# TensorE packing, a merged column sum and shifted copies in a scan, attention and convolution kernel

## The chip, the cores and the metric

The kernel runs on one core of a Trainium2 chip. The core has a matrix engine (TensorE, PE in the profile), a vector engine (VectorE, DVE), an activation engine (ScalarE, ACT), a general engine (GpSimd, POOL) and a queue engine (SyncE, SP). Each works through its own instructions in order; semaphores tie them together. DMA transfers are issued from the queues of POOL, SP and ACT. The metric is the device time of one execution in microseconds (us); the median of several runs is compared.

## The reference

Four layers are applied to an input of 8 images, 384 channels, 32 x 32 pixels, all in float32:

```python
# layer 0: normalise over channels, selective scan forwards and backwards, local gate
xn = x * rsqrt(mean(x*x, channels) + 1e-6) * norm_w
u, z = split(xn_flat @ in_proj.T);  u = silu(conv1d(u))
dt, Bm, Cm = split(u @ x_proj.T, [24, 40])
delta = softplus(dt @ dt_proj.T + dt_b)
h = exp(delta * A) * h + delta * u * Bm          # 16 states a channel, 1024 steps
y = (sum(h * Cm) + u * D) * silu(z);  g = y @ out_proj.T      # both directions
x = x + res_scale * (g * scale_mod + sigmoid(dwconv3(xn)) * xn)
# layer 1: conv branch, linear attention, MLP
x1 = conv1x1(dwconv3(conv1x1(x))) + x
qp, kp, v = phi(q(x1)), phi(k(x1)), v(x1)        # phi(t) = exp(t - t*t/2), 8 heads of 48
out = qp @ (kp.T @ v) / (qp @ sum(kp, pixels) + 1e-6)
x2 = x1 + proj(out);  x = x2 + mlp(layernorm(x2))
# layer 2: seven depthwise kernels (all fit into 13 x 13), summed
# layer 3: 1x1 conv + residual, 13 x 13 depthwise, gelu
```

## The kernel before, in words

The kernel is one program over all 8 images, in three stages.

**Rounds.** `_layers01` runs a loop over the images (line 1036). Round b runs the scan of image b (`scan`, line 678) and, between its 48 units, pieces of two generators: `front(b+1)` (line 554), all of layer 0 ahead of the scan for the next image, and `layer1(b-1)` (line 840), the whole of layer 1 for the image before. Round 0 has `fold()` beside it, round 1 `prepare()`, which builds the 13 x 13 kernels of the last two layers. Each `yield n` of a generator names a cost; the loop takes pieces in such a measure that all are used up when the scan ends (lines 1039, 1041, 1051: `front` counts 108, `layer1` 310). A planner (the tile framework) then fixes, ahead of the run and from its own estimates of durations, the order of the instructions on each engine: the earlier in the program, the higher the priority, among those that it takes to be ready. Buffers are handed out from pools of fixed size: 11 tiles `t2` of 128 x 512, three PSUM banks `mm` for short sums, three `mo` for long ones, two `acc` for the scan.

A scan unit is 4 exponentials on ACT (line 754), three passes of DVE over 128 x 2048 or 2052 elements (767, 691, and the scan itself in 774 or 777), and 8 matmul instructions on PE (693) that sum 4 states of 32 channels each in four column tiles of 32. A float32 matmul is two instructions.

The parts of the generators that the change touches:

- `front`, mean square: three squares on ACT, a matmul of each with `mean_w` (128 x 128, all 1/384, line 565), which leaves the mean on all 128 partitions; `rsqrt` (548) takes Ln and Exp on 128 x 512; DVE multiplies (570). `layer1` does the same for the variance (984 to 994).
- `front`, `xd`: for each direction d, three matmuls of 128 x 56 weights (637), a copy on ACT and a store of B and C. Then for each d three matmuls with only 24 contracted rows (650), Abs, Relu, Exp and Ln on ACT, and sums and stores (`deltas`, 663).
- `layer1`, k and v: for each 128 pixels, kp and vt are computed; four matmuls of 128 x 96 weights add v'k to the PSUM tile `kvs` (902), and three with a column of ones add the sums of kp in three further columns (906). `kv` and `ks` are read from `kvs` by DVE (912, 919).
- `layer1`, denominator: `den`, `rz` and `rzb` (951 to 965) on partitions 0 to 31.

**Convolutions.** `conv` (line 282) runs twice, as a and b, each time over 96 groups of 4 channels. Rows of 32 pixels of all 8 images lie behind each other in DRAM, with `PADW` zeros between them. For every four groups a tile `xt` (two buffers) is loaded by two POOL DMAs (295) of 64 partitions each: the same rows twice, the second shifted by one pixel, so that two horizontal taps are contracted in one matmul. For every two groups four DMAs of SP and ACT load the kernels `toep` (302). A group is 14 matmuls of 64 columns (312), into the two halves of one PSUM bank; `put2` (321) copies it out on DVE and ACT in turn and stores every four groups, `put3` (361) applies gelu on ACT and stores each group.

**Pointwise.** Between the two convolutions, 16 steps of a 1x1 conv (lines 336 to 357).

Of the kernel before, what the change touches and what calls it, by code (L numbers as in the profile page):

```python
# [39 lines left out]
PADW = KS - 1  # L40
# [23 lines left out]
def tile_layers(  # L64
# [39 lines left out]
    RL = PADW + B * (W + PADW)  # L104
# [144 lines left out]
    XL = RL - PADW // 2 - 6  # L249
    with tc.tile_pool(name="cw", bufs=1) as cwp, tc.tile_pool(name="cx", bufs=2) as cxp, tc.tile_pool(  # L250
# [31 lines left out]
        def conv(t_d, src_d, tag, put):  # L282

            xt = tp = None
            for g in range(NQ):
                if g % GB == 0:
                    xt = cxp.tile([P, 2 * GB, XL], FP, tag="xt", name=f"xt_{tag}_{g}")
                    for q in range(2):  # L290
                        src = bass.AP(
                            src_d.tensor, src_d[4 * g, 0, PADW - KS // 2 + q].offset,
                            [[RL, 2 * H], [2 * H * RL, 2 * GB], [1, XL]],
                        )
                        nc.gpsimd.dma_start(xt[2 * H * q : 2 * H * (q + 1)], src)  # L295
                ps = cps.tile([P, HALF], FP, tag="cv", name=f"cv_{tag}_{g}")
                if g % (GB // 2) == 0:
                    tp = toep[g // (GB // 2) % len(toep)]
                    for q in range(2):
                        for e in range(2):  # L300
                            lo = 2 * H * q + H * e
                            (nc.scalar if e else nc.sync).dma_start(
                                tp[lo : lo + H, :, e].rearrange("p g j t -> p g (j t)"),
                                t_d[2 * g : 2 * g + GB, lo : lo + H, :].rearrange("g p n -> p g n"),
                            )
                for t in range(KP // 2):
                    for e in range(2):
                        row = xt[:, 2 * (g % GB) + e, 2 * t : 2 * t + B * (W + PADW) - PADW]
                        rhs = bass.AP(
                            row.tensor, row.offset, [row.ap[0], [W + PADW, B], [1, W]]  # L310
                        )
                        nc.tensor.matmul(  # L312
                            ps[2 * H * e : 2 * H * (e + 1), 0:BW], tp[:, 2 * (g % (GB // 2)) + e, :, :, t].rearrange("p c j -> p (c j)"), rhs,
                            start=(t == 0), stop=(t == KP // 2 - 1), skip_group_check=True,
                        )
                put(g, ps[:, 0:BW])
# [19 lines left out]
        for t in range(H // 2):  # L336
            yt = cxp.tile([P, NC, NB], FP, tag="yp", name=f"yp_{t}", bufs=3)
            nc.sync.dma_start(yt, yf[:, :, t * NB : (t + 1) * NB])
            xo = xos[t % 3]
            for m in range(NC):  # L340
                ps = cps.tile([P, HALF], FP, tag="cv", name=f"pw_{t}_{m}")
                for k in range(NC):
                    nc.tensor.matmul(  # L343
                        ps[:, 0:NB], pwt[:, k, m * P : (m + 1) * P], yt[:, k, :],
                        start=(k == 0), stop=(k == NC - 1),
                    )
                tm = cxp.tile([P, NB], FP, tag="tm", name=f"tm_{t}_{m}", bufs=3)
                nc.scalar.activation(
                    tm, ps[:, 0:NB], AF.Identity, bias=pbias[:, m, :], scale=bns("pw", m)
                )  # L350
                for r in range(2):
                    mid = xo[:, m, r, PADW:RL].rearrange("p (b w) -> p b w", w=W + PADW)[:, :, 0:W]
                    nc.vector.tensor_add(
                        mid, tm[:, r * BW : (r + 1) * BW].rearrange("p (b w) -> p b w", w=W),
                        yt[:, m, r * BW : (r + 1) * BW].rearrange("p (b w) -> p b w", w=W),
                    )
            nc.gpsimd.dma_start(xf[:, :, 2 * t : 2 * t + 2, :], xo)  # L357
# [13 lines left out]
def _layers01(tc, nc, B, xv, x2_d, dram, ident, mean_w, eps5, eps6, one, half, minus1, vec, bns, bnt,  # L371
# [12 lines left out]
    with ExitStack() as ctx:  # L384
# [33 lines left out]
        wx = const(xproj_t.rearrange("(k p) e -> p k e", p=P), [P, NC, DTR + 2 * NST], "wx")  # L418
        wdt = const(dtproj_t, [DTR, C], "wdt")
# [7 lines left out]
        m8t = const(mask8_t, [32, C], "m8t")  # L427
# [22 lines left out]

        ones = wp.tile([P, 1], FP, tag="ones", name="ones")
        nc.vector.memset(ones, 1.0)
# [95 lines left out]
        def rsqrt(dst, ps, eps):  # L548
            nc.scalar.activation(dst, ps, AF.Ln, bias=eps)
            nc.scalar.activation(dst, dst, AF.Exp, scale=-0.5)  # L550
# [3 lines left out]
        def front(b):  # L554

            xn = []
            for h in range(2):
# [3 lines left out]
                stat = psum(f"ms_{b}_{h}")  # L561
                for c in range(NC):
                    sq = t2(f"sq_{b}_{c}_{h}")
                    nc.scalar.activation(sq, xh[:, c, :], AF.Square)
                    nc.tensor.matmul(stat, mean_w, sq, start=(c == 0), stop=(c == NC - 1))
                rstd = t2(f"rstd_{b}_{h}")
                rsqrt(rstd, stat, eps6)
# [43 lines left out]
            for h in range(2):  # L611
# [20 lines left out]
                xds = []  # L632
                for d in range(2):
                    xd = t2(f"xd_{b}_{h}_{d}")
                    ps = psum(f"xd_{b}_{h}_{d}")
                    for k in range(NC):
                        nc.tensor.matmul(
                            ps[: DTR + 2 * NST, :], wx[:, k, :], ucs[d][:, k, :],
                            start=(k == 0), stop=(k == NC - 1),
                        )  # L640
                    nc.scalar.copy(xd[: DTR + 2 * NST, :], ps[: DTR + 2 * NST, :])
                    nc.gpsimd.dma_start(bc_d[b, d][:, cols], xd[DTR : DTR + 2 * NST, :])
                    xds.append(xd)
                    yield 3

                for d in range(2):
                    dls, ts = [], []
                    for c in range(NC):
                        ps = psum(f"dt_{b}_{h}_{d}_{c}")
                        nc.tensor.matmul(  # L650
                            ps, wdt[:, c * P : (c + 1) * P], xds[d][:DTR, :], start=True, stop=True
# [11 lines left out]
                    def deltas(h=h, d=d, dls=dls, ts=ts, ucs=ucs):  # L663
                        for c in range(NC):
                            dl, t = dls[c], ts[c]
# [4 lines left out]
                        if d == 1:  # L670
                            for c in range(NC):
                                nc.vector.tensor_add(ucs[0][:, c, :], ucs[0][:, c, :], ucs[1][:, c, :])
                            nc.gpsimd.dma_start(udv[b][:, :, bass.ts(h, HALF)], ucs[0])

                    defer(1, deltas)
                    yield 6
# [163 lines left out]
        def layer1(b):  # L840
# [37 lines left out]

            wk = wtile(qkv_t[:, C : 2 * C], f"wk_{b}")
            wv = wtile(qkv_t[:, 2 * C : 3 * C], f"wv_{b}")  # L880
            kvs = long_psum(f"kvs_{b}")
            nc.tensor.matmul(kvs[:, 0 : C + NC], zero[:, 0:P], zero[:, 0 : C + NC], start=True, stop=False, skip_group_check=True)
            for t in range(L // P):
# [5 lines left out]
                for w, dst in ((wk, kp), (wv, vt)):  # L889
# [5 lines left out]
                    if w is wk:  # L895
                        phi(kp[:, :C], ps[:, :C], f"k_{b}_{t}")
                    else:
                        nc.scalar.copy(vt[:, :C], ps[:, :C])
                last = t == L // P - 1
                for a in range(NPR):  # L900
                    s = slice(a * PR, (a + 1) * PR)
                    nc.tensor.matmul(
                        kvs[:PR, s], vt[:, s], kp[:, s], start=False, stop=last, skip_group_check=True
                    )
                for c in range(NC):
                    nc.tensor.matmul(
                        kvs[:, C + c : C + c + 1], kp[:, c * P : (c + 1) * P], ones,
                        start=False, stop=last, skip_group_check=True,
                    )
# [6 lines left out]
            )  # L916
            ks = t2(f"ks_{b}")
            ksv = ks[:, 0 : NC * 32].rearrange("p (c e) -> p c e", e=32)
            nc.vector.tensor_mul(
                ksv, m8, kvs[:, C : C + NC].rearrange("p (c o) -> p c o", o=1).to_broadcast([P, NC, 32])  # L920
# [27 lines left out]
            for h in range(2):  # L948
                den = psum(f"den_{b}_{h}")
                for k in range(NC):  # L950
                    nc.tensor.matmul(
                        den[:32, :], ksv[:, k, :], qps[h][:, k, :], start=(k == 0), stop=(k == NC - 1)
                    )
                rz = t2(f"rz_{b}_{h}")
                nc.scalar.activation(rz[:32, :], den[:32, :], AF.Ln, bias=eps6[:32])
                nc.scalar.activation(rz[:32, :], rz[:32, :], AF.Exp, scale=-1.0)
                rzs.append(rz)
                yield 3
            for h in range(2):
                for k in range(NC):  # L960
                    ps = psum(f"rzb_{b}_{h}_{k}")
                    nc.tensor.matmul(
                        ps, m8t[:, k * P : (k + 1) * P], rzs[h][:32, :], start=True, stop=True
# [20 lines left out]
            for h in range(2):  # L984
                xn = xns[h]
                var = psum(f"var_{b}_{h}")
                for k in range(NC):
                    sq = t2(f"vs_{b}_{h}_{k}")
                    nc.scalar.activation(sq, xn[:, k, :], AF.Square)
                    nc.tensor.matmul(var, mean_w, sq, start=(k == 0), stop=(k == NC - 1))  # L990
                rstd = t2(f"rst1_{b}_{h}")
                rsqrt(rstd, var, eps5)
# [43 lines left out]
        for b in range(B):  # L1036
            work = []
            if b + 1 < B:
                work.append([front(b + 1), 108, 0])
# [114 lines left out]
```

## Time and profile before

| | us |
|---|---|
| median of 3 runs (6033.6 to 6047.84) | 6042.61 |
| the profiled execution | 6068.56 |
| its span, first to last instruction | 6066.8 |
| start to the first scan unit | 246 |
| round 0 | 492 |
| round 1 | 944 |
| rounds 2 to 6 (513, 558, 554, 550, 557) | 2732 |
| round 7 | 474 |
| layer 1 of the last image, alone | 366 |
| convolution a | 338 |
| pointwise | 138 |
| convolution b | 337 |

The stages are cut where the last `fr` of a round is computed (line 716) and where the first `xt` of a convolution is issued. PE is busy for 4850.3 us, DVE for 3998.1, ACT for 2852.0, POOL for 1216.0. In the lists of groups a line gives the source line, engine, operation, the tile written and read, the shape and the count; then busy time, the mean duration of one in ns, and the idle time of the engine just ahead of it with what ended it. PE's durations include its pipeline, so that consecutive matmuls overlap: how long a row of them takes is read from the start times in the timeline.

### The profile page before, as it was taken

Reading aid. Unit: us, or ns where it says so; the run is one execution under the profiler, and the core shown is the slowest. Engines: PE = TensorE matmul, PEld = TensorE weight load, DVE = VectorE, ACT = ScalarE, POOL = GpSimd, SP = SyncE. Lnnn points to the kernel's source line nnn. Section 1 sums busy time; section 2 is a strip of 40 time slices with the busy share of each in tenths; the row PEclk is TensorE's granted clock in tenths of the full one; section 3 lists DMA queues with packets and bytes.
Section 4 is the critical chain, followed back from the end, with each engine's and each line's share of the span. In section 5 each row is a group of like instructions: output and inputs, shape, how many; then the busy total and the mean of one; then the engine's idle time right before and its main releaser. Section 6 shows DMA issues by size and latency. Waiting matters only on the chain. (4 is left out here: it accounts for less than half of the span.)

```text
span 6066.8 us, 53234 instructions
## 1 busy us (share of the span) xinstructions
PE 4850.3 (80%) x19054; PEld 2142.6 (35%) x19054; DVE 3998.1 (66%) x2768; ACT 2852.0 (47%) x3941; POOL 1216.0 (20%) x1953
## 2 busy tenths in 40 slices
PE   3665546675479989898998999898978879798899
PEld 1121112222124324232333333242323324497488
DVE  0499995565674897998899789978989921000200
ACT  1555433443435755684577467556735513000211
POOL 4211111222122221212121121211110010211133
PEclk8676767787789989898999899898989979899999
DMA  8655554556473664567457556755663431598799
GB/s 284 202 181 178 181 187 135 167 171 186 139 224 117 192 203 147 170 203 211 143 181 212 157 183 184 213 151 165 199 171 111 142 95 47 111 221 192 220 217 196
DMA packets 429276, 1060.29 MB, mean 175 GB/s; under 512 B 61500, under 2 KB 111908, under 8 KB 429012
## 3 DMA queue, kind: packets, MB, share of 16 engines
q0 software_dynamic: 188640, 679.21, 39.0%
q1 hardware_dynamic: 210704, 354.31, 18.8%
q10 hardware_dynamic: 29668, 23.36, 1.6%
q8 instruction: 151, 2.47, 0.2%
q14 instruction: 113, 0.93, 0.1%
HBM read 807.16 MB, written 293.47 MB: 181 GB/s over the span
## 5 line engine op out<-in xcount | busy, mean ns | idle before, releaser
L754 ACT ACTIVATE da<-dlt,neg_a 128x512 f32<-128x512 f32 x1536 | 1005.2, 713 | 1061.3 <-DVE du L774 570.3
L767 DVE TENSOR_TENSOR du<-vr,bct 128x2048 f32<-128x2048 f32 x384 | 875.2, 2284 | 46.9 <-DMA vr<-v_d 41.0
L691 DVE TENSOR_TENSOR du<-du,bct 128x2048 f32<-128x2048 f32 x384 | 877.2, 2286 | 4.1 <-DVE xx L972 0.3
L777 DVE TENSOR_TENSOR_SCAN du<-da,du 128x2052 f32<-128x2052 f32 x192 | 848.8, 4427 | 13.9 <-ACT da L754 8.5
L774 DVE TENSOR_TENSOR_SCAN du<-da,du 128x2052 f32<-128x2052 f32 x192 | 848.0, 4426 | 8.5 <-ACT da L754 5.6
L693 PE MATMUL acc<-du,selt 128*32 128x512 f32 x3072 | 570.9, 687 | 324.2 <-DVE du L691 308.4
L1008 PE MATMUL mo<-hm,w 128*128 128x512 f32 x1152 | 568.0, 634 | 130.4 <-ACT hm L1006 129.3
L500 PE MATMUL mf<-ln,w 128*128 128x512 f32 x1152 | 552.3, 617 | 36.9 <-DMA w<-w_d 36.9
L1008 PEld LDWEIGHTS mo<-hm,w 128*128 128x128 f32 x1152 | 218.5, 200 | 474.8 <-issue 236.3
L500 PEld LDWEIGHTS mf<-ln,w 128*128 128x128 f32 x1152 | 214.9, 195 | 365.8 <-issue 326.2
L693 PEld LDWEIGHTS acc<-du,selt 128*32 128x32 f32 x3072 | 92.5, 115 | 681.8 <-DVE du L691 403.8
L312 PE MATMUL cv_b<-xt_b,toep 128*64 128x256 f32 x2688 | 304.5, 387 | 34.7 <-DMA xt_b<-xp_d 16.9
L509 PE MATMUL dw<-dw_i,t3b 96*32 96x512 f32 x1152 | 252.3, 784 | 99.0 <-DMA dw_i<-h_d 87.8
L312 PE MATMUL cv_a<-xt_a,toep 128*64 128x256 f32 x2688 | 302.9, 386 | 30.1 <-issue 24.2
L312 PEld LDWEIGHTS cv_b<-xt_b,toep 128*64 128x64 f32 x2688 | 291.6, 195 | 48.1 <-issue 33.5
L500 PE MATMUL in<-xn,win 128*128 128x512 f32 x576 | 284.2, 628 | 28.8 <-ACT uz L588 22.6
L312 PEld LDWEIGHTS cv_a<-xt_a,toep 128*64 128x64 f32 x2688 | 291.6, 195 | 41.1 <-issue 39.6
L754 ACT ACT_TABLE_LOAD x195 | 250.2, 1283 | 67.3 <-DVE du L777 41.1
L509 PE MATMUL lc<-lc_i,t 96*32 96x512 f32 x1152 | 188.4, 671 | 65.0 <-DMA lc_i<-xn_d 64.2
L1006 ACT ACTIVATE hm<-mf,biasf 128x512 f32<-128x512 f32 x192 | 129.9, 686 | 225.7 <-PE mf L500 224.3
L327 DVE COPY yt<-cv_a 128x256 f32<-128x256 f32 x48 | 20.4, 425 | 309.6 <-PE cv_a L312 309.6
L500 PE MATMUL h<-xx,c 128*128 128x512 f32 x288 | 143.6, 659 | 81.3 <-DMA xx<-x_d 81.3
(212 smaller groups left out, 6353.9 us busy)
## 6 DMA issues: line engine op xcount, KB each, us to landing
dlt<-dl_d SPq DMA_DIRECT2D x384, 256.0 KB, 5.3
vr<-v_d SPq DMA_DIRECT2D x384, 256.0 KB, 5.4
bct<-bc_d SPq DMA_DIRECT2D x256, 256.0 KB, 4.0
ut<-u_d POOLq DMA_DIRECT2D x192, 257.5 KB, 4.7
lc_i<-xn_d POOLq DMA_DIRECT2D x192, 228.8 KB, 4.6
dw_i<-h_d POOLq DMA_DIRECT2D x192, 228.8 KB, 4.2
tp_d<-g_d POOLq DMA_DIRECT2D x64, 672.0 KB, 9.4
w<-w_d POOLq DMA_DIRECT2D x64, 576.0 KB, 5.1
```

The lines of the kernel that those rows point to most:

```text
L312: nc.tensor.matmul(ps[2 * H * e : 2 * H * (e + 1), 0:BW], tp[:, 2 * (g % (GB // 2)) + e, :, :, t].rearrange("p c j -> p (c j)"), rhs, star ...
L327: nc.vector.tensor_copy(hold["t"][:, g % GB, :], ps)
L500: nc.tensor.matmul(ps, w[:, k, m * P : (m + 1) * P], rhs[k] if isinstance(rhs, list) else rhs[:, k, :], start=(k == 0), stop=(k == NC - 1),)
L509: nc.tensor.matmul(ps[32 * j : 32 * j + 32, :], lhs(j, i), rhs(j, i), start=(i == 0), stop=(i == taps - 1), skip_group_check=True,)
L691: nc.vector.tensor_mul(dv, dv, cct[:, 1:2, :].to_broadcast([P, 4, HALF]))
L693: nc.tensor.matmul(acc[32 * j : 32 * j + 32, :], selt, dv[:, j, :], start=False, stop=(r == NR - 1), skip_group_check=True,)
L754: nc.scalar.activation(da[:, SEG * j + 1 : SEG * (j + 1)], dlt[:, j, :], AF.Exp, scale=neg_a[:, 4 * c + j, r : r + 1],)
L767: nc.vector.tensor_mul(flat(1)[:, :, 0:HALF], vt, bct[r][:, 0:1, :].to_broadcast([P, 4, HALF]))
L774: nc.vector.tensor_tensor_scan(du[:, s], da[:, s], du[:, s], 0.0, ALU.mult, ALU.add)
L777: nc.vector.tensor_tensor_scan(du[:, s][:, ::-1], da[:, s][:, ::-1], du[:, s][:, ::-1], 0.0, ALU.mult, ALU.add)
L1006: nc.scalar.activation(hm, ps, AF.Gelu, bias=biasf[:, NC * i + f, :])
L1008: nc.tensor.matmul(acc[m], wb[:, f, m * P : (m + 1) * P], hm, start=(i == 0 and f == 0), stop=(i == FF // C - 1 and f == NC - 1),)
```

## The change

Four things are edited.

1. *Convolutions.* `PADW` falls from 12 to 6, so that neighbouring images share their padding, and a row has 312 elements instead of 364. `xt` is loaded by one DMA into one half of the partitions, and a DVE copy writes the other half, shifted by one element. Which half is loaded alternates (`flip`), and the kernels go to the matching halves.
2. *Mean squares and variances.* `rsqrt_mean` replaces `rsqrt`: twelve matmuls of 128 x 32 weights over 128 columns each put the mean of quarter j of the pixels on partitions 32j to 32j+31; Ln and Exp run on 128 x 128; four matmuls with `spread` bring each quarter back to all partitions, in PSUM, where DVE reads it.
3. *`xd` and `dt`.* The x_proj weights are padded to 64 columns. Both directions write one PSUM tile, in column tiles 0 and 64, and are copied in one go. `wdt` holds the dt weights twice, at partitions 0 and 64, so that the two directions' matmuls use different row tiles; the loop over chunks c is now outside the loop over d, with a yield of 3 for each c. `udv` is stored by chunk. `front` counts 90.
4. *Sums of k.* vt gets a 97th column of ones for each group of 96 (a memset on POOL), and the v'k matmul gives the sums in row 96. At the end of the image that row is copied by ACT, and three matmuls of one row turn it into columns. The denominator moves to partitions 32 to 63, with its mask in the free rows of `wdt`.

```diff
-PADW = KS - 1
+PADW = KS // 2
...
-    RL = PADW + B * (W + PADW)
+    RL = PADW + B * (W + PADW) + 2
...
-    XL = RL - PADW // 2 - 6
+    XL = RL - 1
...
-                    for q in range(2):
-                        src = bass.AP(
-                            src_d.tensor, src_d[4 * g, 0, PADW - KS // 2 + q].offset,
-                            [[RL, 2 * H], [2 * H * RL, 2 * GB], [1, XL]],
-                        )
-                        nc.gpsimd.dma_start(xt[2 * H * q : 2 * H * (q + 1)], src)
+                    flip = g // GB % 2
+                    src = bass.AP(
+                        src_d.tensor, src_d[4 * g, 0, 0].offset,
+                        [[RL, 2 * H], [2 * H * RL, 2 * GB], [1, XL]],
+                    )
+                    half0, half1 = (xt[2 * H * e : 2 * H * (e + 1)] for e in (flip, 1 - flip))
+                    nc.gpsimd.dma_start(half0, src)
+                    nc.vector.tensor_copy(half1[:, :, 0 : XL - 1], half0[:, :, 1:XL])
...
-        def rsqrt(dst, ps, eps):
-            nc.scalar.activation(dst, ps, AF.Ln, bias=eps)
-            nc.scalar.activation(dst, dst, AF.Exp, scale=-0.5)
+        def rsqrt_mean(srcs, eps, name):
+            stat = psum(f"{name}_s")
+            for k, src in enumerate(srcs):
+                for j in range(4):
+                    nc.tensor.matmul(
+                        stat[32 * j : 32 * j + 32, 0:P], mean_w[:, 0:32], src[:, j * P : (j + 1) * P],
+                        start=(k == 0), stop=(k == NC - 1), skip_group_check=True,
+                    )
+            r = t2(f"{name}_r")[:, 0:P]
+            nc.scalar.activation(r, stat[:, 0:P], AF.Ln, bias=eps)
+            nc.scalar.activation(r, r, AF.Exp, scale=-0.5)
+            ps = psum(f"{name}_b")
+            for j in range(4):
+                nc.tensor.matmul(
+                    ps[:, j * P : (j + 1) * P], spread[:, j, :], r, start=True, stop=True,
+                    skip_group_check=True,
+                )
+            return ps
...
-                xds = []
-                for d in range(2):
-                    xd = t2(f"xd_{b}_{h}_{d}")
-                    ps = psum(f"xd_{b}_{h}_{d}")
-                    for k in range(NC):
+                xd = t2(f"xd_{b}_{h}")
+                ps = psum(f"xd_{b}_{h}")
+                for k in range(NC):
+                    for d in range(2):
+                        nc.tensor.matmul(
+                            ps[64 * d : 64 * d + 64, :], wx[:, k, :], ucs[d][:, k, :],
+                            start=(k == 0), stop=(k == NC - 1), skip_group_check=True,
+                        )
+                nc.scalar.copy(xd, ps)
...
+                for c in range(NC):
+                    dls, ts = [], []
+                    for d in range(2):
+                        ps = psum(f"dt_{b}_{h}_{d}_{c}")
+                        at = slice(64 * d, 64 * d + DTR)
                         nc.tensor.matmul(
-                            ps, wdt[:, c * P : (c + 1) * P], xds[d][:DTR, :], start=True, stop=True
+                            ps, wdt[at, c * P : (c + 1) * P], xd[at, :], start=True, stop=True
                         )
...
-                        nc.scalar.copy(vt[:, :C], ps[:, :C])
+                        vv1 = vt[:, : C + NPR].rearrange("p (a e) -> p a e", e=PR + 1)
+                        nc.gpsimd.memset(vv1[:, :, PR : PR + 1], 1.0)
+                        nc.scalar.copy(
+                            vv1[:, :, 0:PR], ps[:, :C].rearrange("p (a e) -> p a e", e=PR)
+                        )
...
-                        kvs[:PR, s], vt[:, s], kp[:, s], start=False, stop=last, skip_group_check=True
-                    )
-                for c in range(NC):
-                    nc.tensor.matmul(
-                        kvs[:, C + c : C + c + 1], kp[:, c * P : (c + 1) * P], ones,
-                        start=False, stop=last, skip_group_check=True,
+                        kvs[: PR + 1, s], vv1[:, a, :], kp[:, s], start=False, stop=last,
+                        skip_group_check=True,
                     )
...
+            nc.scalar.copy(kv[PR : PR + 1, :C], kvs[PR : PR + 1, :C])
+            kss = psum(f"kss_{b}")
+            for c in range(NC):
+                nc.tensor.matmul(
+                    kss[:, c : c + 1], kv[PR : PR + 1, c * P : (c + 1) * P], spread[PR : PR + 1, 3, 0:1],
+                    start=True, stop=True, skip_group_check=True,
+                )
...
-                work.append([front(b + 1), 108, 0])
+                work.append([front(b + 1), 90, 0])
```

## The prediction

> **What bounds the kernel now.** I read first the busy time by stage, then, inside one steady round and inside a convolution, the waits and the timeline, then the rows of the instructions that change. By stage (us; busy time and instructions of PE, weight loads, DVE, ACT, POOL; granted clock, DMA share, GB/s): round 0, one steady round, convolution b.
>
> ```profile
> 246.00:738.00 492.00, 291.22 (x975) 87.73 (x976) 480.62 (x309) 271.71 (x392) 84.63 (x151) 0.67 0.53 177
> 2753.00:3307.00 554.00, 492.78 (x1654) 179.44 (x1650) 492.65 (x316) 356.95 (x479) 113.00 (x193) 0.93 0.60 182
> 5730.00:6067.00 337.00, 304.47 (x2688) 291.56 (x2688) 0.00 (x0) 45.55 (x96) 117.70 (x144) 0.97 0.96 202
> ```
>
> Round 0 is DVE from end to end. In a steady round PE and DVE are both busy for 89%, so each bounds for a part. Where PE bounds is seen in the timeline of that round, DVE's long stalls first, then PE while k'v is summed:
>
> ```profile
> 2857.47 0.69 DVE L873 TENSOR_TENSOR xx<-xx,c 128x512 f32<-128x512 f32 x1 [6.38 <-ACT c L870]
> 2889.03 0.17 DVE L764 COPY du<-carry 128x4 f32<-128x4 f32 x1 [15.42 <-PE acc L693]
> 2921.01 0.17 DVE L764 COPY du<-carry 128x4 f32<-128x4 f32 x1 [4.21 <-PE acc L693]
> ...
> 2879.17 0.92 PE L902 MATMUL kvs<-kp,vt 128*96 128x96 f32 x8
> 2879.93 0.76 PE L906 MATMUL kvs<-ones,kp 128*128 128x1 f32 x6
> 2880.54 1.54 PE L892 MATMUL kv_kp<-wk,xx 128*128 128x384 f32 x4
> 2887.90 1.07 PE L693 MATMUL acc<-du,selt 128*32 128x512 f32 x8
> ```
>
> From 2850 to 2943 PE has hardly a gap, and DVE waits some 25 us there for sums queued behind other PE work. Of the round's 61 us of DVE idle time, the list of waits puts only 23 on `acc`; later stretches (3060 to 3307, where `xd` and `dt` lie) have DVE busy and PE with short gaps. Rows that change:
>
> ```profile
> L650 PE MATMUL dt<-xd,wdt 24*128 24x512 f32 x192 | 106.2, 668 | 5.6 <-DVE biasf L824 5.5
> L637 PE MATMUL xd<-uc,wx 128*56 128x512 f32 x192 | 95.3, 623 | 7.3 <-ACT uc L630 7.3
> L565 PE MATMUL ms<-sq,mean_w 128*128 128x512 f32 x96 | 56.3, 730 | 66.9 <-ACT sq L564 63.4 <-DVE bias L824 3.3
> L906 PE MATMUL kvs<-ones,kp 128*128 128x1 f32 x384 | 48.3, 241 | 0.0
> ```
>
> In convolution b, four groups take PE 12.49 us, and the second of the two row loads is issued 6 us after the first:
>
> ```profile
> 5806.41 0.69 POOL L295 DMA_DIRECT2D xt_b<-xp_d  x1 [1.61 <-PE cv_b L312]
> 5807.09 0.89 POOL L364 DMA_DIRECT2D out<-ot  x1
> 5807.36 12.49 PE L312 MATMUL cv_b<-xt_b,toep 128*64 128x256 f32 x112 [1.25 <-ACT ot L363]
> 5812.42 0.69 POOL L295 DMA_DIRECT2D xt_b<-xp_d  x1
> 5820.19 12.49 PE L312 MATMUL cv_b<-xt_b,toep 128*64 128x256 f32 x112 [0.34 <-issue]
> ```
>
> POOL holds the second load behind two stores of `out`; with 8.0 us to landing (median of these loads) it arrives at about 5820, when PE starts again. PE runs from 5739.2 to 6061.6, 322 us, where 24 x 12.5 = 300 would do; in convolution a from 5265.2 to 5586.9, also 322. The DMA engines are 0.96 and 0.89 busy.
>
> [...] the 8 scan instructions above, four tiles of 32, take 0.99 us to the next start, about as long as two unpacked ones (0.89); no run here shows row tiles. [...]
>
> **The change part by part.** The sum is made against the profiled execution, 6068.56 us, 2 us more than its span and 26 more than the median of the runs; the difference is then taken from the median.
>
> *Convolutions.* Bytes for four groups: rows 2 x 704 KB, now 64 x 8 x 311 x 4 = 622 KB; the kernels stay at 8 x 112. So 2304 KB become 1518, and one POOL issue of 0.69 us goes. New is the DVE copy of 64 x 8 x 310 = 2480 elements a partition: [...] I take 1.45. [...] The four groups in the other buffer hide it for 12.5. In convolution a, `put2` copies are queued behind it on DVE; six PSUM banks, 19 us of groups, cover that wait. Without cover the stall would be the copy, 24 x 1.45 = 35 us a convolution. [...] I leave 0.1 us a tile: 322 becomes 303, 19 saved, twice. The first tile of each: 10.6 and 9.8 us from issue to first matmul now, some 2 less with one load. Together -42. What is late next is PE itself.
>
> *Sums of k.* 64 pixel blocks lose 6 instructions, 0.61 us between starts: 39 us of PE. In the steady rounds this lies in the stretch that PE bounds: 8 x 0.61 = 4.9 a round. Added: 64 memsets on POOL, 0.22 us each by the memsets of line 522, before the ACT copy of vt. If a memset were late, vt, then `kvs`, then the sums behind it would be. POOL waits 9 to 14 us for `z_d` there; but what PE does later cannot stand ahead of a memset that PE's earlier sum needs, so I take 0, with 0 to 1 us a block (64) as bounds. Per image one ACT copy (0.47 as line 932) and six tiny matmuls follow; the projection of kv does not wait for them: 0 to 1.
>
> *`xd` and `dt`.* `xd`: six instructions take 2.66 us (3090.9 to 3093.6), 32 times, 85 us; halved, -43. `dt`: 96 matmuls of about 0.95, -46 if row tiles pair, 0 if not. But DVE bounds that stretch: 0 on the path. ACT gets 6 table loads a half image instead of 4, 32 x 1.28 = 41 us, about 5 a round beside 357 busy of 554; DVE waited 2.0 for `da` in that round. 0, at worst +5 a round. 32 more POOL issues of 0.55 lie on an engine 20% busy.
>
> *Mean squares.* 2.66 us of PE become 24 short instructions, 0.75 to 1.5, and 8 with a full weight load, 0.1 each as in line 906: 1.6 to 2.3; 32 times, -10 to -35, taken -20. ACT's two passes fall from 0.69 and 0.63 to about 0.37 and 0.31 (slope from 384 and 512 elements, 612 and 714 ns). New is that PE, not only DVE, waits for them:
>
> ```profile
> 740.28 1.28 ACT L549 ACT_TABLE_LOAD   x1
> 741.58 0.69 ACT L549 ACTIVATE rstd<-ms,eps 128x512 f32<-128x512 f32 x1
> 742.28 1.28 ACT L550 ACT_TABLE_LOAD   x1
> 743.58 0.63 ACT L550 ACTIVATE rstd<-rstd 128x512 f32<-128x512 f32 x1
> ```
>
> Two loads and two short passes make 3.3 us between `stat` and `spread`. Everything on PE behind `spread` waits unless the planner puts other matmuls in between; in the steady round the matmuls of `h` and `in` stand there now, in a place that they may keep. I take 1 us a round uncovered.
>
> *Sum.* Convolutions -42. PE loses 39 + 43 + 46 + 20 = 148 us of work; on the path: rounds 2 to 6, (4.9 - 1) x 5 = -20; round 1 -6; rounds 0 and 7 -2; last layer 1 alone, -5 + 1 = -4; shorter padding to clear, -1. Total -75: 6068.6 gives 5993.6, the median 6042.6 gives **5968**.
>
> **Rivals.** *Rounds unmoved*: DVE, at 89%, takes nothing of PE's gain; only -42, 6000. For it: most PE savings lie where DVE is busy. Against: 25 us of DVE waiting in the k'v stretch. *PE is the bound*: all 148 and the convolutions count, 6042.6 - 190 = 5853. Against: round 0 and the later half of each round. *Packing does nothing*: row tiles don't pair; that costs 46 us of PE but none of the path, 5970. *Slower, the spread wait*: 32 times PE stands from `stat` to the end of Exp, 3.3 us bare, 6 with four exponentials of the scan (2.6) ahead in ACT's queue. All uncovered, 32 x 6 = 192: 6042.6 - 75 + 192 = 6160. It decides from 75/32 = 2.3 us a time. For it: PE works in order, and in rounds with no gap the scan's sums, then DVE, stand behind it. *Order drawn anew*: round 1 takes 944 us with PE 563 and DVE 629 busy, since the order fixed ahead keeps engines waiting in turn; other piece sizes change every order. Either sign, 30 to 100 us.
>
> **How the numbers follow.** The sum as worked out, paired row tiles or not, 0.40; rounds unmoved 0.17; PE bound or a luckier order 0.11; slower by the spread wait or the order 0.26; gain and loss cancelling 0.06. Three runs spread over 14 us, so 0.2%, 12 us, is about what a measurement can tell. Faster 0.68, same 0.06, slower 0.26. The sum's own range is 5930 to 6010; with rivals of both signs, and the bounds of memsets (+64) and table loads (+35), 5865 to 6110.
>
> **What would show it.** PE in each convolution within 305 us, the copy row near 1.45 us, DMA share below 0.8. Line 906 gone. `xd` at half its PE time. Round 0 unchanged; steady rounds 545 to 553. Wrong if PE shows waits of over 2 us for Exp ahead of `spread`, if vt's copy waits for a POOL memset, or if round 1 leaves 900 to 970.

## The result

The changed kernel takes 6054.62 us (median of 4 runs, 6039.45 to 6061.74), the kernel before 6040.34 in the same comparison (4 runs, 6033.6 to 6047.84): ratio 1.002, 95% interval 0.9997 to 1.0043. That is no change that can be measured. The forecast was 5968. The two profiled executions are the other way round, 6068.56 before and 6039.45 after: the first lies above every timed run of its kernel, the second is the fastest of its own. So stages are read from them for what happens inside, and sums are taken from medians.

The stages of the changed kernel that answer to those shown of before: round 0 (cut, as before, just ahead of the first scan instruction), one steady round, convolution b (columns: start and end, length; busy time and instructions of PE, weight loads, DVE, ACT, POOL; granted clock, DMA share, GB/s).

```profile
232.00:724.00 492.00, 272.25 (x1028) 81.61 (x1025) 468.94 (x304) 270.80 (x384) 88.22 (x159) 0.68 0.53 176
2729.00:3292.00 563.00, 482.62 (x1720) 179.97 (x1720) 491.02 (x315) 354.61 (x477) 116.46 (x207) 0.92 0.58 181
5720.00:6038.00 318.00, 305.37 (x2688) 282.69 (x2688) 37.82 (x24) 45.54 (x96) 108.98 (x120) 0.98 0.71 154
```

Convolution b has lost 19 us, as forecast, with a DMA share of 0.71 instead of 0.96. Round 0 is as long as before. The steady round has 10 us less PE work (482.6 against 492.8) and the same DVE work, and is 9 us longer, not shorter. The gain of both convolutions is there; it is given back in the rounds.

Groups of the changed kernel, in the form of the groups shown of before:

```profile
L316 PE MATMUL cv_b<-xt_b,toep 128*64 128x256 f32 x2688 | 305.4, 389 | 14.0 <-DVE xt_b L298 14.0
L298 DVE COPY xt_b<-xt_b 64x2480 f32<-64x2480 f32 x24 | 37.8, 1576 | 263.5 <-DMA xt_b<-xp_d 263.5
L673 PE MATMUL dt<-xd,wdt 24*128 24x512 f32 x192 | 86.1, 684 | 20.4 <-ACT dl L678 7.3 <-DVE fr L737 5.5 <-DMA x_d<-xx 5.5
L658 PE MATMUL xd<-uc,wx 128*64 128x512 f32 x192 | 60.4, 605 | 1.2 <-ACT uc L651 1.2
L931 PE MATMUL kvs<-kp,vt 128*97 128x96 f32 x512 | 59.0, 260 | 41.9 <-ACT vt L925 30.0 <-POOL vt L924 11.4
L570 PE MATMUL ms_b<-ms_r,spread 128*128 128x128 f32 x128 | 27.7, 384 | 58.4 <-ACT ms_r L567 58.4
```

PE waits in convolution b only for the first copy (14.0 us). `xd` falls from 95.3 to 60.4 us of PE, and the product of 97 rows costs what that of 96 did (260 ns against 255 before). `dt` falls less, from 106.2 to 86.1, because only about half of its 48 pairs (the matmuls of the two directions for one chunk) start together. In the timeline of PE in the same round:

```profile
3264.22 1.12 PE L673 MATMUL dt<-xd,wdt 24*128 24x512 f32 x2
3270.03 1.13 PE L673 MATMUL dt<-xd,wdt 24*128 24x512 f32 x4
```

Four instructions (both directions) take as long as two (one direction): two row tiles do run at once, where the planner leaves them side by side.

### The profile page after: what moved, and what is told of

Same layout as the page of the kernel before. It is cut to its first block, busy times and chain, and to the rows that moved or that the text cites. A ratio compares the mean times of both kernels' runs of the same rounds, so it can differ in the third digit from the quotient of the medians.

```text
span 6037.7 us, 54476 instructions
## 1 busy us (share of the span) xinstructions
PE 4758.3 (79%) x19550; PEld 2101.6 (35%) x19550; DVE 4065.4 (67%) x2815; ACT 2851.9 (47%) x3949; POOL 1212.2 (20%) x2006
## 3 DMA queue, kind: packets, MB, share of 16 engines
q1 hardware_dynamic: 210704, 354.31, 19.5%
## 4 chain that ended last, share of the span: by engine, by line
PE 28%; DVE 24%; issue 23%; DMA 11%; ACT 7%; POOL 4%; SPq 1%; POOLq 0%; DVEq 0%; ACTq 0%
DVE du L798 7%; DVE du L788 6%; DVE du L795 6%; PE cv_a L316 5%; DVE du L712 3%; PE mo L1038 3%; PE mf L508 3%; DMA vr<-v_d 2%; PE in L508 2%; PE acc L714 2%; DMA x_d<-fr 2%; DMA dl_d<-dl 1%; POOL out L368 1%; PE c L508 1%; DMA dw_i<-h_d 1%
## 5 line engine op out<-in xcount | busy, mean ns | idle before, releaser
L714 PE MATMUL acc<-du,selt 128*32 128x512 f32 x3072 | 583.4, 702 | 372.3 <-DVE du L712 357.7
L1038 PE MATMUL mo<-hm,w 128*128 128x512 f32 x1152 | 586.4, 652 | 110.2 <-ACT hm L1036 109.5
L298 DVE COPY xt_b<-xt_b 64x2480 f32<-64x2480 f32 x24 | 37.8, 1576 | 263.5 <-DMA xt_b<-xp_d 263.5
```

Source lines behind the costliest of these rows:

```text
L714: nc.tensor.matmul(acc[32 * j : 32 * j + 32, :], selt, dv[:, j, :], start=False, stop=(r == NR - 1), skip_group_check=True,)
L1038: nc.tensor.matmul(acc[m], wb[:, f, m * P : (m + 1) * P], hm, start=(i == 0 and f == 0), stop=(i == FF // C - 1 and f == NC - 1),)
```

## The experiments

Each kernel was timed beside the kernel before, in five comparisons; it ran 4 to 22 times, and the medians of the kernel before lie between 6035.5 and 6040.2.

### One part at a time

**Convolutions alone.** The kernel before with the row loading and the padding of the change.

```diff
-PADW = KS - 1
+PADW = KS // 2
...
+                    nc.gpsimd.dma_start(half0, src)
+                    nc.vector.tensor_copy(half1[:, :, 0 : XL - 1], half0[:, :, 1:XL])
```

> The kernel before with the new loading of the convolution rows alone (one row load, the copy shifted by one on VectorE, shorter padding); everything between is as before. Theory A (the convolutions gained what was forecast, the rounds gave it back): 6040 - 36 to 42, that is 5998 to 6004, with each convolution at 304 us from first to last matmul. Theory B (the convolutions' gain is not real, since their stages in the changed kernel only look shorter): 6035 to 6045.

Measured: 6083.46, ratio 1.0072 (1.0059 to 1.0084). Both theories fall. Each convolution is 305 or 306 us on PE, as wanted, and the whole is 47 us slower. From the end of round 0 to the first row load of convolution a, the profiled execution takes 4582 us where the kernel before takes 4515.

**The packing alone.** The changed kernel with the old convolutions and the old padding.

```diff
-PADW = KS // 2
+PADW = KS - 1
...
-                    nc.gpsimd.dma_start(half0, src)
-                    nc.vector.tensor_copy(half1[:, :, 0 : XL - 1], half0[:, :, 1:XL])
```

> The changed kernel with the old convolutions: all the packing between the scan rounds, none of the row loading. Theory A: the packing as a whole costs what the convolutions gained, 6080 to 6100. Theory B: the packing is neutral, 6040 +- 12.

Measured: 6028.51, ratio 0.9983 (0.9974 to 0.9992). The packing between the rounds is worth 8 us. So it isn't what gave the gain back: the convolution edit is.

**Sums of k alone.** Lines 904 to 953 of the changed kernel, with a small tile of ones in place of `spread`.

```diff
+                        nc.gpsimd.memset(vv1[:, :, PR : PR + 1], 1.0)
-                for c in range(NC):
-                    nc.tensor.matmul(
-                        kvs[:, C + c : C + c + 1], kp[:, c * P : (c + 1) * P], ones,
```

> The kernel before with k's sums taken in the v'k product alone (a memset of ones in vt, product of 97 rows, six tiny matmuls per image in place of 384 one-column matmuls). The forecast's step (4.9 us a round in five rounds, some in round 1): 6010 to 6020. Rival 1 (the product now waits for vt, some 4.6 us a round in place of the gain): 6035 to 6045. Rival 2 (the waits for vt cost more than the sums): 6055 to 6080.

Measured: 6013.83, ratio 0.9962 (0.9949 to 0.9975): 23 us less, in the range of the forecast's step.

**Means alone.** The denominator moves to partitions 32 to 63 with them.

```diff
-                rsqrt(rstd, stat, eps6)
+                rstd = rsqrt_mean(sqs, eps6, f"ms_{b}_{h}")
```

> The kernel before with the mean squares and reciprocal roots alone done in the packed way (means in four column tiles, exponential on one row of four, spread back by four short matmuls); the mask of the denominator moves into rows 32 to 64 of the dt weights' tile to make room. Theory 1 (the wait ahead of the spread gives the gain back): 52 us of PE waits for it in rounds 2 to 6 of the changed kernel, less some 13 us of PE work saved there: 6070 to 6090. Theory 2 (these waits are only other waits under a new name, since the mean's own PE work shrank): 6030 to 6045. The forecast's step: 6035 to 6045.

Measured: 6049.59, ratio 1.0018 (1.0008 to 1.0029): 13 us slower, below what theory 1 asks and above theory 2. Its 22 runs spread from 6027 to 6069, wider than those of any other kernel here.

**`xd` and `dt` alone.**

```diff
-                for d in range(2):
+                for c in range(NC):
...
-                work.append([front(b + 1), 108, 0])
+                work.append([front(b + 1), 90, 0])
```

> The kernel before with xd and dt alone done in the packed way (both directions in two column tiles and two row tiles, chunks outside the loop over directions, the denominator on partitions 32 to 63). The forecast: none of its PE saving on the path, 6030 to 6045. If the parts of the packing add up (the packing as a whole -8, k's sums -23, the means +13): 6038. Rival (the two more table loads a half image are on the path): 6055 to 6075.

Measured: 6041.18, ratio 1.0006 (0.9997 to 1.0014). Nothing, as forecast; the 25 more table loads (666 against 641 in all) don't show. The three parts add up to -23 + 13 + 2 = -8, as much as the packing measures as a whole.

### Which part of the convolution edit: loading or layout

In the kernel with the convolution edit alone the instructions of PE, ACT and SP stand in the same order as in the kernel before, one by one (PE's neighbours in different tiles, which run side by side, as the eight of a scan unit do, 0.99 us to the next start in the kernel before, start up to four places apart); DVE has only the copies added, and on POOL a few issues near 90 us, ahead of round 0, have changed places. The order of work can't be the cause. What is left: the new loading reaches back, or the rows of `x2_d`, which layer 1 writes in every round and which are now 312 elements long instead of 364, with 6 zeros between images instead of 12.

```diff
 PADW = KS - 1
 RL = PADW + B * (W + PADW)
...
+                    nc.gpsimd.dma_start(half0, src)
+                    nc.vector.tensor_copy(half1[:, :, 0 : XL - 1], half0[:, :, 1:XL])
```

> The kernel before with one row load and the shifted copy, but with the old padding of 12 and the old row length of 364. Theory A1 (the new row layout slows the stores of layer 1's output, 32 runs of 128 bytes in each DMA packet, and through them the rounds): the rounds stay as in the kernel before and the convolutions gain, 5995 to 6005. Rival A2 (something in the new loading itself reaches back into the rounds): about 6080 as the full convolution edit.

```diff
-PADW = KS - 1
+PADW = KS // 2
...
                     for q in range(2):
                         nc.gpsimd.dma_start(xt[2 * H * q : 2 * H * (q + 1)], src)
```

> The kernel before with the new padding of 6 and row length of 312, but with two row loads as before. Theory A1: the rounds of the full convolution edit, some 65 to 70 us longer, with convolutions near the old 322 us (12% fewer bytes, a few us less): 6090 to 6110. Rival A2: 6030 to 6040.

Measured: new loading on old rows 5996.11, ratio 0.9934 (0.9916 to 0.9952); new rows with the old loading 6077.27, ratio 1.0071 (1.0054 to 1.0089). The loading is worth 39 us. The row layout costs 83 us with the new loading (1.0072 against 0.9934). Convolution b of the kernel with new rows and old loads (the same columns as above) shows why its total is lower than was expected:

```profile
5758.00:6073.00 315.00, 296.50 (x2688) 289.03 (x2688) 0.00 (x0) 45.50 (x96) 118.23 (x144) 0.98 0.94 204
```

With 12% fewer bytes in the row loads, and two of them, it is as short (301 us from the first matmul to the last) as with one load on old rows. Either half of the edit frees the convolutions, so this kernel shows the cost of the rows less that gain.

How the layout costs time is seen in POOL's timeline at the end of round 5. First new loading on old rows, then the full convolution edit:

```profile
3828.44 3.50 POOL L1024 DMA_DIRECT2D x_d<-xx  x3 [1.98 <-DVE xx L1021]
3841.26 0.56 POOL L721 DMA_DIRECT2D x_d<-fr  x1 [1.75 <-DVE fr L720]
3846.88 0.75 POOL L849 DMA_DIRECT2D xx<-x_d  x1 [5.06 <-DMA x_d<-fr]
```

```profile
3871.81 3.50 POOL L1024 DMA_DIRECT2D x_d<-xx  x3 [1.98 <-DVE xx L1021]
3884.64 0.56 POOL L721 DMA_DIRECT2D x_d<-fr  x1 [1.75 <-DVE fr L720]
3897.98 0.76 POOL L849 DMA_DIRECT2D xx<-x_d  x1 [12.78 <-DMA x_d<-fr]
```

In both, the first line is three stores of layer 1's output to `x2_d` (each is 2048 runs of 32 pixels, 128 bytes; the last three of the kernel before went out in 192 packets of 4096 bytes, 32 runs each). The last `fr` of the round is stored 12.8 us later, and then POOL waits for it to land, since layer 1 of the next image reads it back as `xx`. On old rows the wait is 5.1 us, on new rows 12.8: a store of `fr` that is issued behind slow stores lands late itself. What PE pays, in the lists of waits from round 1 into the last layer 1, in the same order of kernels:

```profile
PE h L504 <- DMA xx<-x_d: 78.7, 8, 15.4
PE c L513 <- DMA ut<-u_d: 1.4, 1, 1.4
PE ms L569 <- ACT sq L568: 7.1, 2, 6.7
```

```profile
PE h L504 <- DMA xx<-x_d: 116.3, 7, 20.8
PE c L513 <- DMA ut<-u_d: 29.2, 4, 10.1
PE ms L569 <- ACT sq L568: 17.6, 2, 14.9
```

(Columns: us in total, times, the longest.) These three grow by 38, 28 and 11 us, and the list as a whole from 785 to 855, while the stretch up to convolution a grows from 4501 to 4582 us. All are loads that land late, the third by way of `xi`, which the squares read (ACT waits 39 us for it instead of 30).

### Alignment or row length

The stores of `x2_d` in the kernel with the full convolution edit, image by image (windows around the six stores of images 1, 3, 4 and 7 in turn; columns: count, KB each, median us from issue to landing):

```profile
x_d<-xx POOLq DMA_DIRECT2D x6, 256.0 KB, 13.7
x_d<-xx POOLq DMA_DIRECT2D x6, 256.0 KB, 6.3
x_d<-xx POOLq DMA_DIRECT2D x6, 256.0 KB, 17.3
x_d<-xx POOLq DMA_DIRECT2D x6, 256.0 KB, 6.0
```

Images 0, 2, 5 and 6 have 19.5, 14.3, 16.2 and 13.6. In the same windows the stores of `fr` land in 5.3 us behind image 3 and in 14.1 to 18.6 behind images 1, 2, 4 and 5. The run (32 pixels) of image b begins 24 + 152b bytes into a row, and a row has 1248 bytes, a multiple of 32. So, if the tile itself begins at a multiple of 32 bytes, all runs of images 3 and 7, and of no other image, do so too. In the changed kernel, with the same rows, images 3 and 7 have 7.4 and 6.0, the others 11.3 to 22.7. In the kernel before (48 + 176b, rows of 1456) one run in two is aligned, in every image: 9.2 to 15.2 us. If alignment is the cause, a padding of 8 (32 + 160b, rows of 1312) repairs all images, and a padding of 16 puts every run at a multiple of 64.

```diff
-PADW = KS // 2
+PADW = 8
-    RL = PADW + B * (W + PADW) + 2
+    RL = PADW + B * (W + PADW)
-    XL = RL - 1
+    XL = B * (W + PADW) - PADW + KS
-                        src_d.tensor, src_d[4 * g, 0, 0].offset,
+                        src_d.tensor, src_d[4 * g, 0, PADW - KS // 2].offset,
```

> The changed kernel with a padding of 8 instead of 6 (row length 328), so that each run of 128 bytes in the rows of layer 1's output starts at a multiple of 32 bytes, half of them at one of 64. Theory A1 in the form that alignment is the cause: the rounds of the packing alone with old rows, or better, and the new convolutions: 5960 to 5990. Rival A3 (the row pitch or the place in DRAM is the cause, not the alignment): 6030 to 6060, like the changed kernel.

> The changed kernel with a padding of 16 (row length 400), every run of 128 bytes at a multiple of 64 bytes. If 64 bytes are the unit that matters: 5950 to 5980 and shorter packets than with padding 8. If 32 bytes are: within 8 us of padding 8, a little above it for the longer row loads and copies (3040 elements a partition instead of 2480). Rival A3: 6030 to 6060.

Measured: padding 8: 5953.57, ratio 0.9866 (0.9841 to 0.9891); padding 16: 5958.38, ratio 0.9878 (0.9855 to 0.99). The changed kernel with nothing but this padding is 1.3% faster than the kernel before. Rival A3 falls. The order of work is not a rival here: the packing alone, the changed kernel and these two share one order, up to the same small swaps as above; the kernel before, both halves of the convolution edit, the edit as a whole and the convolutions with a padding of 8 (below) share another. 32 bytes are enough: with padding 16 the stores take 7.1 us to land, with padding 8 (stores of rounds 2 to 6):

```profile
x_d<-xx POOLq DMA_DIRECT2D x30, 256.0 KB, 7.0
x_d<-fr POOLq DMA_DIRECT2D x30, 256.0 KB, 5.4
```

In the changed kernel as it is these two lines read 17.1 and 16.3. The waits appear at other places than in the convolution edit alone, since the order of work is another one. Waits of PE and DVE in rounds 1 to 7 of the changed kernel, first with a padding of 8, then as it is:

```profile
PE ms_s L561 <- ACT sq L587: 20.0, 8, 6.7
PE acc L769 <- DMA y<-ud_d: 17.9, 6, 7.6
DVE du L788 <- DMA vr<-v_d: 21.9, 9, 7.5
```

```profile
PE ms_s L561 <- ACT sq L587: 51.9, 7, 13.4
PE acc L769 <- DMA y<-ud_d: 44.2, 8, 15.5
DVE du L788 <- DMA vr<-v_d: 50.1, 12, 16.4
```

These waits grow by 32, 26 and 28 us. The second and third are loads that land late. The first is a store: a square takes the buffer of a `dl` tile whose store to `dl_d` has not landed; ACT waits 33 us for that in three places, and with a padding of 8 not at all.

The boundary of 32 bytes is what these runs show, for the start of each run in an ordinary store: in the kernel with the full convolution edit, 6.0 to 6.3 us for aligned runs of 128 bytes, 13.6 to 19.5 for unaligned ones. The size of the runs costs little here: with a padding of 8, aligned runs of 128 bytes land in 7.0 us where the 2048-byte rows of `fr`, in stores of the same 256 KB, take 5.4. What fills the extra time of an unaligned store, no run shows.

### What the packing is worth on aligned rows

Three kernels with a padding of 8: the convolutions alone; with k's sums; with k's sums, `xd` and `dt` (the changed kernel without its packed means).

> The kernel before with the new row loading and a padding of 8: no packing. If alignment is worth as much to the old rounds as to the packed ones (5954 against 6028 less 38): 5996 - 37, that is 5950 to 5970. If the old rounds, which have another order of work, hide more of it: 5975 to 5995.

> As the last, with k's sums in the v'k product too. If both gains add: 5930 to 5945, below every kernel so far. If the gain of k's sums was in the same waits that alignment removed: 5950 to 5965.

> The changed kernel with a padding of 8 and without the packed means (mean squares and reciprocal roots as before). If the packed means cost 13 here too: 5940 against 5954 with them. If they cost only in the old order of work: 5950 to 5960. Against the kernel without the packing of xd and dt it tells what that is worth in this place; forecast 0.

Measured: 5967.26 (0.9889, 0.9872 to 0.9905); 5946.81 (0.9848, 0.9835 to 0.9862); 5916.41 (0.9802, 0.9781 to 0.9822). Against old rows, alignment is worth 5996 - 5967 = 29 us without any packing. K's sums give 20 again. `xd` and `dt`, worth nothing before, are worth 30 here, and the means cost 5954 - 5916 = 37. Neither was forecast. The sums of k hardly change the order of the rest: of 18142 matmul instructions that both kernels have, 526 stand more than four places away.

### The packed means: wait or order

With a padding of 8, first only the front's means packed, then only those of layer 1, then both with a fixed tile in place of the exponential's result (this edit is shown; it leaves out the use of the means):

```diff
-                    ps[:, j * P : (j + 1) * P], spread[:, j, :], r, start=True, stop=True,
+                    ps[:, j * P : (j + 1) * P], spread[:, j, :], mean_w, start=True, stop=True,
```

> The changed kernel with a padding of 8, and of the packed means only those of the front (layer 0's mean square); layer 1's variance as before. Between 5916 (no packed means) and 5954 (both). If the cost lies in the wait ahead of the spread: the front's spreads waited 41 us in rounds 2 to 6 of the kernel with both, layer 1's 14, so three quarters of the 37 here: about 5944. If the order of work is the cause: anywhere between, not in proportion to the waits.

> The same with the packed variance of layer 1 alone. By the waits: 5916 plus a quarter of 37, about 5926. If the order of work is the cause: not in proportion.

> The changed kernel with a padding of 8, in which the spread multiplies a fixed tile of 128 x 128 instead of the exponential's result: all instructions are there, but PE has nothing to wait for at the spread (what is left out is the use of the computed means). If the wait is the cause of the 37: 5910 to 5925. If the order of work, or the work itself, is: 5940 to 5960; but the planner also draws the order anew, so that only a value near 5954 speaks clearly.

Measured: 5935.06 (ratio 0.9828, 0.9815 to 0.9842), 5965.01 (0.9876, 0.9863 to 0.989) and 5875.23 (0.9729, 0.9716 to 0.9743). The part with the shorter waits at the spread (16 us in rounds 2 to 6 of its kernel, against 38) costs more (49 us) than the part with the longer ones (19), and more than both together (37). So the waits at the spread don't give the size of the loss. Without the dependency the kernel is faster than any other, but DVE's wait for the roots is gone too and the planner drew another order, so the difference can't be put down to PE's wait.

Controls of the order alone: the kernel without packed means, at other weights of the front in the loop that deals out its pieces.

```diff
-                work.append([front(b + 1), 90, 0])
+                work.append([front(b + 1), 108, 0])
```

> The kernel with a padding of 8 and no packed means, with the front's weight in the loop back at 108 instead of 90: no instruction is added or taken away, only the places of the pieces between the scan units move. It shows what the order alone is worth: if within 6 us of 5916, differences of 15 and more between the other kernels are not chance of the order; if it moves by 15 or more, they can be.

> The changed kernel (with the packed means) with a padding of 8 and the front's weight at 108. If the packed means cost some 37 us by themselves (the wait): 5941, 37 above the same kernel without them, 5904. If the 37 is chance of the order: anywhere from 5890 to 5960, with a difference far from 37.

> The kernel with a padding of 8 and no packed means, with the front's weight at 120: a second draw of the order alone, beside 5916 (weight 90) and 5904 (weight 108). If the order alone is worth some 12 us: 5895 to 5925. If it is worth several tens: outside that.

Measured: weight 108: 5904.08 (0.9782, 0.9769 to 0.9796); weight 120: 5969.68 (0.9878, 0.9861 to 0.9894); weight 108 with packed means: 5930.1 (0.9814, 0.9799 to 0.983). With the same work (but for table loads, of which the fastest has the most: 700, 658 and 672), the weights 108, 90 and 120 give 5904, 5916 and 5970: the order alone is worth up to 66 us. The packed means cost something in all five places where they can be compared (13, 19, 26, 37 and 49 us), but each of these is within what a new order can do, and so are the 30 us of `xd` and `dt`, which are 43 at a weight of 108 and a loss of 23 at 120. Whether the wait ahead of the spread or the order sets the cost of the means stays open.

The kernel with weight 108 and without packed means, 5904 us, is the fastest of those that leave nothing out: 2.2% below the kernel before.

## Why the prediction was wrong

**Convolutions, -42: right.** The new loading on old rows gives 6035.5 - 5996.1 = 39 us. The copy takes 1447 ns in convolution a and 1446 to 1846 in b (the 1.45 us taken for it was the author's assumption, no trace of the kernel before shows such a copy); the new row loads land in 7.1 to 7.4 us (medians of the changed kernel; single ones in 5.6 to 8.7), so that landing and copy together, some 9 us, lie within the 12.5 us that four groups took before; each convolution has 304 or 305 us of PE, the forecast's line was 305. POOL's issues and the copy hold each other up, both ways: in convolution b 7 of the 96 issues of `out` take 1.5 to 2.2 us instead of 0.89, each ending 0.48 us after a copy that it overlaps, and 13 of the 24 copies, which begin 0.29 to 0.62 us into such an issue, take up to 0.40 us longer. PE doesn't wait for that.

**The step that failed: "shorter padding to clear, -1".** The padding was followed to where it is cleared and to where rows are read, and not to where they are written: six stores of `x2_d` by layer 1 of every image, in the middle of the rounds. Of a changed layout every writer counts as well as every reader. This term was priced at -1 us; on the kernel before, with the new loading, it is +83. In the changed kernel it is what remains: the change measures +14, the packing -8 and the loading -39 by themselves, so by subtraction the rows cost some 62. (The padding of 8 takes off 101, since it also ends what half-aligned rows cost the kernel before.) None of the rivals named it. The slower rival was given 0.26 for a wait at the spread or a new order; what slowed the kernel needed neither.

**Sums of k: right in kind, somewhat too large.** Of 39 us of PE, 4.9 a steady round, 24 in five, were expected on the path, and more in the other stages; alone they give 23, on aligned rows 20. The memsets on POOL were bounded at 64 us and taken as 0. No copy of vt waits for one in the changed kernel, so that sign of being wrong stayed away; PE does once, 11.4 us, and its waits for the copy of vt rose (30.0 us against 7.2 before). The gain came all the same.

**`xd` and `dt`: right on the kernel before, +2 for 0.** Row tiles pair, so "-46 if row tiles pair" is partly met (20 us of busy time, since the planner parts many of the pairs). Of the 32 more table loads that were expected 25 came; they cost nothing that can be seen.

**Means: -20 of PE, 1 us a round uncovered, taken as nearly nothing: too good.** Their busy time on PE falls by 15 us (113 to 98), and they cost 13 us alone. In a row the 24 short instructions take 0.68 to 1.48 us to the next start (0.75 to 1.5 was the author's estimate), the 8 with `spread` 0.99 to 2.01 (0.8 was taken). The waits are far above 1 us a round: in rounds 2 to 6 of the changed kernel PE waits 36.6 us for the exponential in the front and 15.3 in layer 1, that is 10 us a round, 2.6 a time on average and up to 7.2. The rival was to decide from 2.3 us a time; but the time of the kernel doesn't follow these waits.

**The sum.** The changed kernel with a padding of 8 takes 5954 where 5968 was forecast. That is luck in part: the forecast had -42 for the convolutions and -33 for the rest, and the parts measured on aligned rows are -39 (loading), -29 (alignment, in no term), -20 (sums of k), -30 (`xd` and `dt`, taken as 0) and +37 (means, taken as nearly 0).

**What would show it.** The signs named for the convolutions came true, line 906 is gone, and round 0 is unchanged (492 us). `xd` came down to 63% of its PE time, not to half. The steady rounds left 545 to 553 (555 to 565 in rounds 3 to 6), and PE waited more than 2 us ahead of the spread, which was named as a sign against. The last two pointed to the rounds, and neither to the cause: with a padding of 8 the same waits are there (41.1 and 14.0 us) and rounds 3 to 6 take 549 to 553.

**"Order drawn anew, 30 to 100":** real as an effect, 66 us between three orders of the same work; but not what took the forecast gain, since the layout costs its time at an unchanged order.

## What to carry to other kernels

When a layout in DRAM changes, work out the start of every run that is written, modulo 32 bytes, before its size; stores of short runs that begin off such a boundary took two to three times as long here (13.6 to 19.5 us against 6.0 to 6.3) and went with late landings of what was issued behind them (stores of `fr` 14.1 to 18.6 us against 5.3), in a stage whose own code the edit doesn't touch. When one edit of a large program disappoints, put its parts one by one on the old kernel, above all the part that seems to work: here the gain and the loss came from the same edit. In a program whose order is fixed by a planner, compare several orders of the same work first; a part that is worth less than their spread can't be judged from one.

## What was not expected of the hardware

Stores of 256 KB in runs of 128 bytes landed in 6.0 to 6.3 us where all runs began at a multiple of 32 bytes, in 9.2 to 15.2 where one in two did, and in 13.6 to 19.5 where none did (medians of an image's six stores; with a padding of 8, all aligned, 5.2 to 7.5, and 11.3 for image 0, which is the slowest in each of these kernels); multiples of 64 brought nothing more (7.1 against 7.0). A DVE copy of float32 from one half of the partitions to the other, 2480 elements each, took 1447 ns. Such a copy and a DMA issue of POOL did not overlap freely: an issue of 0.89 us took up to 2.16 beside a copy, and a copy up to 1.85 us beside an issue. Two matmuls with 24 contracted rows in row tiles 0 and 64 took 1.13 us for four instructions, as long as two alone.
